# Short matrix products split in two within each period: adapters and weighted values first, output projection, then scores and mixing

## The chip, the cores and the metric

The kernel runs on one core of a Trainium2 chip. The metric is the device time in microseconds of one execution on that core, median of several runs. The core has five engines that work side by side and wait for each other by semaphores: TensorE (PE, matrix products into PSUM banks; PEld is its loading of weights), VectorE (DVE), ScalarE (ACT), GpSimd (POOL) and SyncE (SP), which here issues nearly all transfers.

## The reference

All data are 32-bit floats. `x` holds 128 sequences of 32 tokens with 512 channels. What is computed, cut to its steps:

```python
h = einsum('bct,bcd->bdt', x, cond_weights[cond])      # mixes the 32 tokens of a sequence
q, k, v = split(clip(h @ w_qkv.T, -8, 8))              # 512 channels each
q, k = layernorm(q) * qw + qb, layernorm(k) * kw + kb
s = q @ k.T / 4 + alibi_bias, causal                   # 32 heads of 16 channels, within a sequence
x = x + (softmax(s) @ v) @ w_out.T
h = x @ adapt_w[adapter].T                             # one 512x512 matrix for each sequence
gs = sum(top2(h @ gate_w))
y = relu(h @ up_w)**2 @ down_w + gs * (h @ fc1_w @ expert_w @ fc2_w)
out = x + layernorm(y) * gamma + beta
```

## The kernel before

The 4096 tokens are cut into 32 tiles of 128 tokens (`NTILE`), four sequences each; two neighbouring tiles make a pair (`GRP` = 2) for the feed-forward part. The loop at line 815 is software-pipelined by hand: one pass over its body is a period, and period t works on tile t + 2 (projections to q, k, v), tile t + 1 (scores, softmax), tile t (weighted values, output projection), tile t - 1 (adapter product), tile t - 2 (routing) and the pair before (up products in even t, down products in odd t). Tiles 0 to 3 are led in by the code from line 702 on.

In a period of the kernel before, TensorE's steps come in this order. The short ones use part of the array or few columns:

- `scores(t + 1)` (L439): 32 products on 64 rows x 32 columns of the array into the two banks `psc`; VectorE then adds the bias into `s`.
- `mix(t + 2)` (L301): from tile 5 on, 32 products on 64 x 32 into two banks `pxc` (the "parts"); ScalarE copies them to `xcT`. For the first tiles, `t <= 2 * GRP`, it is four 128 x 128 products into one bank instead.
- `adapt(t - 1)` (L559): 64 products on 128 x 32 into `pad`; VectorE transposes them to `hT`. The weights `adw` come by eight transfers of 512 KB (`load_adapters`, L255), which wait for `last_head`, the last such transpose.
- `weigh(t)` (L514): 32 products on 128 x 32 into `po`; VectorE transposes them to `aT`.

The rest is on the whole array, 128 x 128:

- `route(t - 2, 0)` (L585), four products into `pr`, from which `gs` and a part of `y` come;
- `fill(0)`, then `project(t + 2, 0)` and `project(t + 2, 1)` (q and k, L328) with `normalise` (L355) and `turn` (L402) behind them: `turn` transposes in blocks on VectorE, sends the blocks to memory and fetches them back turned, by one transfer `away_qk` and four `T_qk`;
- `attend(t)` (L536), the output projection `pw` from `aT`, which VectorE adds to `x`, and `turn_x(t)` (L549), which turns the new `x` the same way (`away_x`, four `T_x`) for the next period's `adapt` and lets GpSimd add beta to `x`;
- `fill(1)` to `fill(3)`, `project(t + 1, 2)` (v), `spread` (L499, GpSimd), `scale(t + 2)` (L413, ScalarE and VectorE, makes `kx` for the next period's scores), `route(t - 2, 1)`, `fill(4)` to `fill(7)`. One `fill` is four up products (`up`, L612, into `pu`) or two down products (`down`, L630, into `pd`). ScalarE applies relu to each `pu` and GpSimd squares it; VectorE adds `pd` to `y` (`total`, L641) and `finish` (L651) normalises.

The softmax is in `exponent` (L464: maximum on VectorE, subtraction on GpSimd, exp on ScalarE), `share` (L475: sum on VectorE, division on GpSimd) and `flip` (L487: transpose to `pT`, which `weigh` of the next period reads).

A 32-bit product of this kernel is two weight loads and two matmuls, four instructions, in TensorE's queue. The framework puts instructions in order for every engine by a schedule of its own; `after` (L77) fixes an order between two instructions of one engine without a wait. `short` chains all short products in the order of the code, and `queue` ties a long product behind the last instruction put there. `idle_instructions(n)` puts n instructions that do nothing behind the last product. `fill_up` calls it at seven places of a period, behind fill(0), the two projections, `attend` and fill(1) to fill(3); the seven share `FIRST` = 117 in period 2, and `SHORT` = 95 in even and 13 in odd periods:

```python
lack = FIRST if t == GRP else SHORT[t % GRP]
idle_instructions(lack // 7 + (i < lack % 7))
```

`last_scale` (L371, L434, L624) fixes one order on ScalarE: the relu of `fill(4)` comes behind the last scaling of q in `scale`.

Of the kernel before, what the change touches and what calls it, by code (L numbers as in the profile page):

```python
# [13 lines left out]
AF = mybir.ActivationFunctionType  # L14
# [3 lines left out]
P = 128  # L18
# [3 lines left out]
NTILE = NT // P  # L22
# [5 lines left out]
FC = INT // P  # L28
# [5 lines left out]
GRP = 2  # L34
ROUT = (0, NE + D // 2, NE + D)


SHORT = (95, 13)
FIRST = 117
CLIP = 8.0  # L40
EPS = 1e-5
NEG = -1.0e30
# [3 lines left out]
def adaln_attn_ffn(  # L46
# [22 lines left out]
    nc = tc.nc  # L69
# [4 lines left out]
    def bank(name):  # L74
        return ps.tile([P, 512], F32, tag="ps", name=name)

    def after(ins, first):  # L77

        tc.add_manual_dep(
            ins.ins, first.ins.name,  # L80
            mybir.DependencyInfo(mybir.DependencyClass.NoSync, mybir.DependencyReason.DATA),
            reason="order",
        )
# [10 lines left out]
    queue = []  # L94
    shorts = []

    def idle_instructions(n):

        for _ in range(n):
            nop = nc.tensor.nop("fill")  # L100
            after(nop, queue[-1])
            queue[:] = [nop]

    def product(*args, **kwargs):
        ins = nc.tensor.matmul(*args, **kwargs)  # L105
        if queue:
            after(ins, queue.pop())
        return ins

    def short(*args, **kwargs):  # L110

        ins = product(*args, **kwargs)
        if shorts:
            after(ins, shorts[-1])
        shorts[:] = [ins]
        return ins
# [184 lines left out]
    def mix(t):  # L301

        s = tiles[t]
        s["xcT"] = w2.tile([P, DC, P], F32, tag="xcT", name=f"xcT_{t}")
        blk = s["blk"].rearrange("p a b -> p (a b)")
        if t <= 2 * GRP:
            pxc = bank(f"pxc_{t}")
            for c in range(DC):
                nc.tensor.matmul(  # L309
                    pxc[:, ts(c, P)], lhsT=s["x"][:, ts(c, P)], rhs=blk, start=True, stop=True  # L310
                )
            nc.scalar.copy(s["xcT"].rearrange("p c n -> p (c n)"), pxc)
            return

        n = P // 2
        banks = [bank(f"pxc_{t}_{r}").rearrange("p (c n) -> p c n", c=DC) for r in range(2)]
        for c in range(DC):
            for g in range(DC):
                for r in range(2):
                    short(  # L320
                        banks[r][ts(g, S), c, :n],
                        lhsT=s["x"][ts(r, n), c * P + g * S : c * P + (g + 1) * S],
                        rhs=blk[ts(r, n), ts(r, n)], start=True, stop=True,
                    )
        for r in range(2):
            nc.scalar.copy(s["xcT"][:, :, ts(r, n)], banks[r][:, :, :n])
# [41 lines left out]

    last_flip = []
    last_head = []  # L370
    last_scale = []  # L371

    def swap(srcs, name):

# [38 lines left out]
    def scale(t):  # L413

        s = tiles[t]
        q, k = s["T"][:, :, 0], s["T"][:, :, 1]

        s["kx"] = w1.tile([P, DC, SEQ, HQ, S], F32, tag="kx", name=f"kx_{t}")
        for c in range(DC):
            nc.scalar.activation(  # L420
                k[:, :, c], s["raw"][1][:, :, c], AF.Identity,
                bias=lnc[:, 3, c : c + 1], scale=lnc[:, 2, c : c + 1],
            )
            kx = nc.vector.tensor_tensor(  # L424
                out=s["kx"][:, c],
                in0=k[:, :, c].unsqueeze(2).broadcast_to([P, SEQ, HQ, S]),
                in1=m_half.unsqueeze(1).unsqueeze(3).broadcast_to([P, SEQ, HQ, S]),
                op=ALU.mult,
            )

            if c == 0 and last_flip:
                after(kx, last_flip[-1])
        for c in range(DC):
            last_scale[:] = [nc.scalar.activation(  # L434
                q[:, :, c], s["raw"][0][:, :, c], AF.Identity,
                bias=qaff[:, 1, c : c + 1], scale=qaff[:, 0, c : c + 1],
            )]

    def scores(t):  # L439

# [171 lines left out]
    def up(g, f):  # L612

        pair = pairs[g]
        pu = bank(f"pu_{g}_{f}")
        for c in range(DC):
            last = product(
                pu[:, : GRP * P], lhsT=up_sb[:, c, ts(f, P)], rhs=pair["hT"][:, c, :],
                start=(c == 0), stop=(c == DC - 1),
            )  # L620
        a = hp.tile([P, GRP * P], F32, tag="act", name=f"act_{g}_{f}")
        relu = nc.scalar.activation(a, pu[:, : GRP * P], AF.Relu)  # L622

        if f == FC // 2 and last_scale:  # L624
            after(relu, last_scale.pop())
        nc.gpsimd.tensor_tensor(out=a, in0=a, in1=a, op=ALU.mult)  # L626
        pair["acts"].append(a)
        return last

    def down(t, quarter):  # L630
        s = tiles[t]
        if quarter == 0:
            s["pd"] = bank(f"pd_{t}")
        for f in range(2 * quarter, 2 * quarter + 2):
            last = product(
                s["pd"], lhsT=pairs[t // GRP]["acts"][f][:, ts(t % GRP, P)],
                rhs=down_sb[:, f, :], start=(f == 0), stop=(f == FC - 1),
            )
        return last
# [74 lines left out]
    routed_outer(0)  # L714
    routed_outer(1)
    mix(0)
    routed_outer(2)
    for c in range(DC):
        for i in range(2):
            project(0, i, (c,))  # L720
    normalise(0)
    mix(1)
    project(0, 2)
    wqkv_dma = dma
# [29 lines left out]
    project(1, 0)  # L754
    turn(0)
    scale(0)
    spread(0)
    project(1, 1)
# [3 lines left out]
    routed_outer(3)  # L762
    blend(2)
    mix(2)
    turn(1)
    project(1, 2)
    share(0)
    project(2, 0)
    scale(1)
    flip(0)  # L770
    blend(3)
# [14 lines left out]
    project(3, 0)  # L786
    share(1)
    scale(2)
    adapt(0)
    flip(1)  # L790
# [18 lines left out]
    def when(ok, step, *args):  # L809
        if ok:  # L810
            step(*args)
# [3 lines left out]
    for t in range(GRP, NTILE + GRP):  # L815
        here, ahead, two = t < NTILE, t + 1 < NTILE, t + 2 < NTILE
        g = t // GRP - 1

        def fill(i):
            last = up(g, i) if t % GRP == 0 else down(g * GRP + i // 4, i % 4)  # L820
            queue[:] = [last]
            if i < 4:
                fill_up(i)

        def fill_up(i):

            if here:
                lack = FIRST if t == GRP else SHORT[t % GRP]
                idle_instructions(lack // 7 + (i < lack % 7))

        when(t == GRP, adapt, t - 1)
        when(ahead, scores, t + 1)
        when(two and t > GRP, mix, t + 2)
        when(GRP < t <= NTILE, adapt, t - 1)
        when(here and t > GRP, weigh, t)
        when(ahead, exponent, t + 1)
        if here:


            load_adapters(t, last_head[-1])  # L840
        if t == GRP:
            after(
                nc.sync.dma_start(out=gam_sb, in_=gamma.broadcast_to([P, D])),
                last_adapter_dma[-1],
            )
        when(t + 3 < NTILE, load, t + 3)
        when(t > GRP and t % GRP == 0, finish, t - GRP - 1)
        when(t > GRP, route, t - GRP, 0)
        when(t == GRP, mix, t + 2)
        fill(0)  # L850
        when(two, project, t + 2, 0)
        fill_up(4)
        when(ahead, share, t + 1)
        when(t + 3 < NTILE, gather, t + 3)
        when(two, project, t + 2, 1)
        fill_up(5)
        when(ahead, flip, t + 1)
        when(two, normalise, t + 2)
        when(two, turn, t + 2)
        when(here, attend, t)  # L860
        fill_up(6)
        when(here, turn_x, t)
        fill(1)
        fill(2)
        fill(3)
        when(t % GRP, total, g * GRP)
        when(ahead, project, t + 1, 2)
        when(ahead, spread, t + 1)
        when(t + 3 < NTILE, blend, t + 3)
        when(t % GRP, finish, g * GRP)  # L870
        when(two, scale, t + 2)
        when(t > GRP, route, t - GRP, 1)
        if t == NTILE + GRP - 1:
            close(NTILE - 1)
            break
        for i in range(4, 8):
            fill(i)
        when(t % GRP, total, g * GRP + 1)
# [77 lines left out]
```

## Time and profile before

| what | us |
|---|---|
| median of 3 runs | 1236.95 (1235.41 to 1237.29) |
| the profiled execution | 1238.49 |
| its span, first to last instruction | 1236.7 |
| TensorE matmuls busy | 1226.7 (99%) |
| weight loads, which lie beside matmuls | 792.1 (64%) |
| VectorE busy | 685.1 (55%) |
| GpSimd busy | 456.9 (37%) |
| ScalarE busy | 330.4 (27%) |
| granted TensorE clock, mean | 0.999 of full |

The profile gives for each group of instructions its engine, the line of the code, output and inputs by name, the shape, how many, the busy time and the idle time before it with what ended that. Matmuls overlap by their run-in and run-out, so the distance from one start to the next tells more than a duration. "issue" as the end of an idle time means that no semaphore and no transfer of the profile ended it.

The largest groups on TensorE are the projections `pqkv` (340.3 us in 768 matmuls), `pu` (228.7), `pd` (220.4), `pr` (125.8), `pad` (121.3 in 4096), `pw` (115.3), `po` (38.3 in 2048), `psc` (37.3 in 2048) and `pxc` in parts (24.5 in 1728). A period takes a little over 37 us.

### The profile page before, as it was taken

What the parts mean: (1) busy time and instruction counts of PE and PEld (TensorE: products, weight loads), DVE (VectorE), ACT (ScalarE), POOL (GpSimd) and SP (SyncE); (2) the same over time, 40 slices, a digit from 0 to 9 for tenths busy, and PEclk for the clock granted to TensorE, in tenths of its full rate; (3) what the DMA queues carried; (4) which work ended last, traced back from release to release, by engine and by line L of the source; (5) the groups of instructions that cost most, each with busy time, mean ns of one, the idle gap of its engine ahead of it and who ended that gap; (6) DMA issues with size and microseconds to landing.
All of it is one profiled execution on the core that took longest, in us unless ns stands there. A gap on an engine that the chain in (4) does not pass through costs nothing.

```text
span 1236.7 us, 32576 instructions
## 1 busy us (share of the span) xinstructions
PE 1226.7 (99%) x13126; PEld 792.1 (64%) x13126; DVE 685.1 (55%) x1090; ACT 330.4 (27%) x675; POOL 456.9 (37%) x393
## 2 busy tenths in 40 slices
PE   9999999999999999999999999999999999999998
PEld 5576566674666756567665666746667566675765
DVE  2975555655556565564645646455565655656222
ACT  2433223231222322133222232222323222231111
POOL 3435334443333524234343343433344243342410
PEclk9999999999999999999999999999999999999999
DMA  9754544335544345544355443455443554533440
GB/s 281 222 196 169 205 189 164 133 135 205 206 165 171 119 165 206 192 169 146 116 202 206 180 167 119 152 206 204 149 159 123 190 205 177 180 114 141 176 157 18
DMA packets 93430, 209.53 MB, mean 169 GB/s; under 512 B 11749, under 2 KB 42470, under 8 KB 93286
## 3 DMA queue, kind: packets, MB, share of 16 engines
q1 hardware_dynamic: 89142, 198.39, 45.3%
q0 software_dynamic: 3424, 8.39, 1.8%
q8 instruction: 110, 1.80, 0.6%
q10 hardware_dynamic: 720, 0.66, 0.2%
q14 instruction: 34, 0.28, 0.1%
HBM read 176.47 MB, written 30.93 MB: 168 GB/s over the span
## 4 chain that ended last, share of the span: by engine, by line
PE 99%; DMA 0%; issue 0%; DVE 0%; ACTq 0%; DVEq 0%
PE pqkv L105 27%; PE pu L105 18%; PE pd L105 17%; PE pad L105 10%; PE pr L592 10%; PE pw L105 9%; PE psc L105 3%; PE po L105 3%; PE pxc L105 2%; PE pro L216 1%; PE pd L676 1%; DMA fc_t<-in_fc_w 0%; PE pxc L309 0%; PE pt L399 0%; PE pe L206 0%
## 5 line engine op out<-in xcount | busy, mean ns | idle before, releaser
L105 PE MATMUL pqkv<-wqkv_sb,xcT 128*128 128x512 f32 x768 | 340.3, 592 | 0.0
L105 PEld LDWEIGHTS pqkv<-wqkv_sb,xcT 128*128 128x128 f32 x768 | 145.5, 190 | 168.6 <-issue 159.0
L105 PE MATMUL pu<-hT,up_sb 128*128 128x256 f32 x1024 | 228.7, 379 | 0.0
L105 PE MATMUL pd<-down_sb,act 128*128 128x512 f32 x496 | 220.4, 592 | 0.0
L105 PEld LDWEIGHTS pu<-hT,up_sb 128*128 128x128 f32 x1024 | 194.5, 190 | 33.4 <-issue 7.7
L424 DVE TENSOR_TENSOR kx<-T_qk,m_half 128x512 f32<-128x512 f32 x128 | 138.0, 1137 | 55.8 <-ACT T_qk L420 55.8
L105 PEld LDWEIGHTS pd<-down_sb,act 128*128 128x128 f32 x496 | 94.2, 190 | 105.6 <-issue 103.6
L505 POOL TENSOR_TENSOR vx<-v,msk 128x1024 f32<-128x1024 f32 x64 | 134.3, 2123 | 59.9 <-DVE v L346 51.2
L468 POOL TENSOR_TENSOR s<-s,mx 128x1024 f32<-128x1024 f32 x32 | 67.1, 2097 | 169.6 <-DVE mx L467 169.6
L592 PE MATMUL pr<-rout_sb,hT 128*128 128x256 f32 (+1 forms) x512 | 125.8, 389 | 0.0
L105 PE MATMUL pad<-adw,T_x 128*32 128x128 f32 x4096 | 121.3, 273 | 2.4 <-issue 1.8
L626 POOL TENSOR_TENSOR act<-act 128x256 f32<-128x256 f32 x128 | 89.8, 710 | 88.7 <-ACT act L622 88.5
L105 PEld LDWEIGHTS pad<-adw,T_x 128*32 128x32 f32 x4096 | 111.3, 110 | 9.2 <-issue 6.0
L105 PE MATMUL pw<-wout_sb,aT 128*128 128x512 f32 x256 | 115.3, 593 | 0.0
L592 PEld LDWEIGHTS pr<-rout_sb,hT 128*128 128x128 f32 x512 | 94.7, 190 | 29.0 <-issue 15.0
L483 POOL TENSOR_TENSOR s<-s,rden 128x1024 f32<-128x1024 f32 x32 | 61.3, 1916 | 89.5 <-DVE gs L601 80.5
L346 DVE TENSOR_SCALAR qk<-pqkv 128x512 f32<-128x512 f32 x64 | 44.1, 689 | 78.6 <-PE pqkv L105 78.2
L105 PEld LDWEIGHTS pw<-wout_sb,aT 128*128 128x128 f32 x256 | 48.5, 190 | 60.9 <-issue 60.4
L557 POOL TENSOR_TENSOR x<-x,bet_sb 128x512 f32<-128x512 f32 x32 | 40.7, 1273 | 119.0 <-DVE blocks_x L380 116.7
L622 ACT ACTIVATE act<-pu 128x256 f32<-128x256 f32 x128 | 47.0, 379 | 136.3 <-PE pu L105 136.3
L491 DVE STREAM_TRANSPOSE pT<-s 128x1024 f32<-128x1024 f32 x32 | 39.8, 1245 | 61.1 <-POOL s L483 61.1
L294 POOL TENSOR_TENSOR blk<-cw,msk 128x128 f32<-128x128 f32 x32 | 12.8, 401 | 150.6 <-DMA cw<-in_cond_w,rows 135.6
(79 smaller groups left out, 1074.5 us busy)
## 6 DMA issues: line engine op xcount, KB each, us to landing
adw<-in_adapt_w SPq DMA_DIRECT2D x256, 512.0 KB, 7.8
away_qk<-blocks_qk SPq DMA_DIRECT2D x28, 512.0 KB, 2.6
T_qk<-away_qk SPq DMA_DIRECT2D x112, 128.0 KB, 2.9
x<-in_x SPq DMA_DIRECT2D x32, 256.0 KB, 10.4
away_x<-blocks_x SPq DMA_DIRECT2D x30, 256.0 KB, 2.7
T_x<-away_x SPq DMA_DIRECT2D x120, 64.0 KB, 2.5
out<-y POOLq DMA_DIRECT2D x30, 256.0 KB, 2.8
wqkv_sb<-in_w_qkvT SPq DMA_DIRECT2D x12, 256.0 KB, 5.6
```

Source lines behind the costliest of these rows:

```text
L105: ins = nc.tensor.matmul(*args, **kwargs)
L294: nc.gpsimd.tensor_tensor(out=s["blk"], in0=s["cw"].unsqueeze(1).broadcast_to([P, SEQ, S]), in1=m_seq.unsqueeze(2).broadcast_to([P, SEQ, S ...
L346: nc.vector.tensor_scalar(out=s["qk"][:, i, :] if i < 2 else s["v"], in0=s["pp", i], scalar1=-CLIP, scalar2=CLIP, op0=ALU.max, op1=ALU.min,)
L424: kx = nc.vector.tensor_tensor(out=s["kx"][:, c], in0=k[:, :, c].unsqueeze(2).broadcast_to([P, SEQ, HQ, S]), in1=m_half.unsqueeze(1).unsqu ...
L468: nc.gpsimd.tensor_tensor(out=s["s"], in0=s["s"], in1=mx.unsqueeze(2).broadcast_to([P, H, S]), op=ALU.subtract,)
L483: s["shared"] = nc.gpsimd.tensor_tensor(out=s["s"], in0=s["s"], in1=rden.unsqueeze(2).broadcast_to([P, H, S]), op=ALU.mult)
L491: pT = nc.vector.transpose(out=s["pT"].rearrange("p h q -> p (h q)"), in_=s["s"].rearrange("p h k -> p (h k)"),)
L505: nc.gpsimd.tensor_tensor(out=vx, in0=s["v"][:, ts(half, D // 2)].rearrange("p (h d) -> p h d", d=HD).unsqueeze(2) .broadcast_to([P, H // ...
L557: nc.gpsimd.tensor_tensor(out=s["x"], in0=s["x"], in1=bet_sb, op=ALU.add)
L592: nc.tensor.matmul(pr[:, :n], lhsT=hT[:, c, ts(t % GRP, P)], rhs=rout_sb[:, c, ROUT[half] : ROUT[half + 1]], start=(c == 0), stop=(c == DC ...
L622: relu = nc.scalar.activation(a, pu[:, : GRP * P], AF.Relu)
L626: nc.gpsimd.tensor_tensor(out=a, in0=a, in1=a, op=ALU.mult)
```

## The change

Period t now begins with `adapt(t - 1)` and `weigh(t)`; `route(t - 2, 0)` follows, then `attend(t)` and `turn_x(t)`, which move up from behind the projections; then `scores(t + 1)`, `mix(t + 2)` and `exponent(t + 1)`, and behind these fill(0) and the rest in the old order. The special order of period 2 goes, but for one tie: there `attend` is placed behind the last short product. `mix` works in parts from tile 4 on, not from tile 5. The idle instructions are shared among six places (the one behind `attend` is gone): none in period 2, 57 in even and 58 in odd periods. `last_scale` goes.

```diff
-SHORT = (95, 13)
-FIRST = 117
+SHORT = (57, 58)
+FIRST = 0
...
-        if t <= 2 * GRP:
+        if t < 2 * GRP:
...
-    last_scale = []
...
-            last_scale[:] = [nc.scalar.activation(
+            nc.scalar.activation(
                 q[:, :, c], s["raw"][0][:, :, c], AF.Identity,
                 bias=qaff[:, 1, c : c + 1], scale=qaff[:, 0, c : c + 1],
-            )]
+            )
...
-        relu = nc.scalar.activation(a, pu[:, : GRP * P], AF.Relu)
-
-        if f == FC // 2 and last_scale:
-            after(relu, last_scale.pop())
+        nc.scalar.activation(a, pu[:, : GRP * P], AF.Relu)
...
-                idle_instructions(lack // 7 + (i < lack % 7))
-
-        when(t == GRP, adapt, t - 1)
-        when(ahead, scores, t + 1)
-        when(two and t > GRP, mix, t + 2)
-        when(GRP < t <= NTILE, adapt, t - 1)
+                idle_instructions(lack // 6 + (i < lack % 6))
+
+        when(t <= NTILE, adapt, t - 1)
         when(here and t > GRP, weigh, t)
-        when(ahead, exponent, t + 1)
         if here:
...
             load_adapters(t, last_head[-1])
...
         when(t > GRP and t % GRP == 0, finish, t - GRP - 1)
         when(t > GRP, route, t - GRP, 0)
-        when(t == GRP, mix, t + 2)
+        if t == GRP:
+            queue[:] = [shorts[-1]]
+        when(here, attend, t)
+        when(here, turn_x, t)
+        when(ahead, scores, t + 1)
+        when(two, mix, t + 2)
+        when(ahead, exponent, t + 1)
         fill(0)
         when(two, project, t + 2, 0)
         fill_up(4)
...
         when(two, turn, t + 2)
-        when(here, attend, t)
-        fill_up(6)
-        when(here, turn_x, t)
         fill(1)
```

## The prediction

> **What bounds the kernel now.** I read the page's busy times and chain first, then the periods of the loop one by one, then TensorE's order of time inside a period.
>
> ```profile
> PE 1226.7 (99%) x13126; PEld 792.1 (64%) x13126; DVE 685.1 (55%) x1090; ACT 330.4 (27%) x675; POOL 456.9 (37%) x393
> ...
> q8 instruction: 110, 1.80, 0.6%
> ...
> PE 99%; DMA 0%; issue 0%; DVE 0%; ACTq 0%; DVEq 0%
> ```
>
> TensorE is the chain, almost without a break; no other engine passes 55%. So only two things can move the time: spaces between TensorE's own instructions, and a wait that does not exist today. The second row returns below. Next the periods, cut at each first `psc` (scores), which in this kernel opens a period:
>
> ```profile
> 571.13:608.56 37.43, 37.43 (x402) 21.19 (x401) 21.46 (x34) 9.27 (x18) 12.01 (x9) 1.00 0.48 170
> 533.43:571.13 37.70, 37.70 (x434) 27.40 (x433) 21.75 (x34) 11.11 (x24) 16.82 (x15) 1.00 0.48 170
> 117.08:156.88 39.80, 38.02 (x401) 21.26 (x401) 21.96 (x35) 9.27 (x18) 13.49 (x11) 1.00 0.45 160
> ```
>
> The second column is the length. 37.43 us is the shortest, met again and again for odd and even t: I call it clean. The 27 periods from t = 3 (117.08) to t = 29 (ending 1136.74) take 1019.66 us, 27 x 37.43 = 1010.61, so 9.05 us are lost: 2.37 in t = 3, 0.70 in t = 4, 5.98 in the other 25. That is all the change can win in the loop.
>
> ```profile
> 117.08 1.16 PE L105 MATMUL psc<-kx,T_qk 64*32 64x128 f32 x64
> 117.98 0.91 PE L105 MATMUL pxc<-blk,x 64*32 64x64 f32 x64
> 118.82 0.42 PE L105 MATMUL pad<-adw,T_x 128*32 128x128 f32 x6
> 120.99 3.57 PE L105 MATMUL pad<-adw,T_x 128*32 128x128 f32 x121 [1.75 <-issue]
> ```
>
> **Where the 9.05 us go.** In t = 3 the adapter products stop after six, released by "issue": no engine, no DMA. I numbered the records of TensorE's queue in order of start. This stop is at record 2498; others, of 0.1 to 0.4 us, are at 3522, 4545, 10690, 14274, 17858. All leave 193 or 194 when divided by 256. The instruction queue's 110 packets of 1.80 MB are 16.4 KB each, one for 256 of the queue's 28,213 records. The packet before the big stop starts at 118.76 and work resumes 2.23 us later; at 463.07 and 613.58 it is 2.38 and 2.46. The adapter weights had landed by 103.2 and `T_x` by 112.8, so once the block is in time nothing is late behind it. So a stop is an instruction block that comes late: 256 records that run through in under some 3.4 to 3.9 us (117.1 to 120.99; 274 to 530 records after the first `psc` in the usual odd period) outrun the next. Today one period begins with 640 dense records (scores 128, mix 128, adapters 256, weigh 128) in 6.3 us, so two block borders always lie close.
>
> Beside the Trainium skill's page "Runtime: NRT & Kernel Launch", section "Instruction fetch mechanics", this row disagrees: the page says blocks of 256 instructions stream in and crossing a border is mostly hidden. By the page the stops would be nothing, the change would win nothing and the estimate would be some 7 us higher.
>
> **The idle instructions.** Odd t has 400 loads, 400 matmuls, 13 idle, 11 waits = 824 records; even t 432 + 432 + 95 + 9 = 968; together 1792 = 7 x 256, so borders stay put. Afterwards 1664 + 115 = 1779; with 13 waits that is 1792 again, and I assume it. The first `pad` of t = 2 starts at record 1510. The changed t = 2 holds adapters 256, output projection 16, scores 128, mix 128, products 176, no idle ones, some 8 waits: 712. So t = 3 begins at 2222 and its borders are 20, 276 and 532 records in; even periods, about 865 later, have them at 180, 436, 692. 20 to 276 looks close, but in the usual odd period today a border 18 records into `psc` starts its packet 2.3 us ahead of the first `psc` (493.66 against 496.00), since the queue is read ahead during long matmuls. 276 to 532 and 180 to 436 now hold routing and output projection (1.88 + 3.43 us). I expect no full stop. Borders inside dense work still cost 0.10 to 0.15 (`pxc` to `pad` 0.25 instead of 0.145 in several even periods); two such in 14 odd periods, at 0.06 on average, 1.7 us. Bounds: 0 to 6.0, today's loss kept. An idle instruction takes 0.071 us of the queue; ten behind fill(0) are 0.7 us under 1.72 us of matmuls, hence nothing. At t = 30, where no projection separates the places, today's 40 take 2.9 us, and `pu` and `pw` run 0.23 long (1.88 for 1.73, 3.51 for 3.43); 29 take 2.0, so 0.23 is won.
>
> **The extra split.** Removing nothing from TensorE, the change cuts the dense run in two, and small array shapes are entered and left twice.
>
> ```profile
> 526.47 7.03 PE L105 MATMUL pd<-down_sb,act 128*128 128x512 f32 x16
> 533.43 1.16 PE L105 MATMUL psc<-kx,T_qk 64*32 64x128 f32 x64
> 534.32 0.91 PE L105 MATMUL pxc<-blk,x 64*32 64x64 f32 x64
> 535.16 3.78 PE L105 MATMUL pad<-adw,T_x 128*32 128x128 f32 x125
> ...
> 539.88 2.05 PE L592 MATMUL pr<-rout_sb,hT 128*128 128x264 f32 x8
> 541.76 1.89 PE L105 MATMUL pu<-hT,up_sb 128*128 128x256 f32 x8
> 543.49 7.03 PE L105 MATMUL pqkv<-wqkv_sb,xcT 128*128 128x512 f32 x16
> 550.35 3.60 PE L105 MATMUL pw<-wout_sb,aT 128*128 128x512 f32 x8
> ```
>
> Read differences of starts. Entering: `pd` x16 takes 6.96 where 16 long ones take 6.86, so 0.09 (0.522 instead of 0.429 at the last). 64x32 to 128x32: the last `pxc` to `pad` takes 0.145 instead of about 0.01: 0.14. Leaving: the last `po` to `pr` takes 0.15, and `pr` needs 1.88 where 1.73 x 264/256 = 1.78 would do: 0.10 more. Afterwards, entering at `pad` costs the 0.09 that `psc` costs today; `pad`, `po`, `pr` are as now; new are entering at `psc` (0.09) and leaving after `pxc` (0.25, taken from `po`, which is also 64 wide; gone is its 0.14). Sum +0.20 us a period, 29 periods (t = 2 to 30): +5.8. No row shows `pxc` to fill(0): leaving the wider `psc` for the big `pxc` at 88.4 cost 0.30, so the upper end is 0.25 a period, 7.3; at the lower the leaving is free, 0.09 - 0.14 = -0.05, -1.5. I take 0.20, by the row of equal width.
>
> The Trainium skill, "TensorEngine Tiling (Array Packing)", section "Key Properties", states that changing the tiling mode drains the engine. It speaks against this change; it gives no figure, so the rows above price it. By rule and by row one more leaving and entering is paid.
>
> **The moved steps, queue by queue.** Zero below counts from the first `pad`.
>
> ```profile
> 576.63 0.72 DVE L578 STREAM_TRANSPOSE hT<-pad 128x512 f32<-128x512 f32 x1 [1.76 <-PE pad L105]
> 577.52 0.72 DVE L529 STREAM_TRANSPOSE aT<-po 128x512 f32<-128x512 f32 x1 [0.17 <-PE po L105]
> ```
>
> *Output projection* (8 matmuls, 3.43) needs `aT`, 0.72 us of VectorE after the last `po`; today project covers it for 10 us, afterwards only `pr`, 2.03 from the last `po`. It is ready about 1.0 after that, so it costs 0 with 0.6 to spare for the weight load. *turn_x*: VectorE add 0.69 and transpose 0.67 run at about 10.1, before the scores come; SP's `away_x` queues behind the eight adapter loads (the last of them lands 13.7 us after the first issue) and holds SP until about 20; SP's next client, `away_qk`, comes at about 26, and `T_x` is needed at 37.6. GpSimd's add, 1.27, ends before the maximum. All hidden. *Scores and exponent*: adds 1.28, maximum 1.22, GpSimd 1.91, exp 1.06, sum 1.22, GpSimd 1.91, transpose 1.25 end near 22; weigh needs them at 41. They delay normalise by some 3 us against today, so `T_qk` lands near 33.5 and `kx` ends near 37 to 39; scores wait until 47.8. *Mix*: two ScalarE copies, 0.65, against fill(0), 1.82: 0. The `last_scale` order goes; whichever of relu and scale comes first, scores have 9 us. Bounds of all this: 0, and what the second rival prices.
>
> **Sum.** The profiled execution took 1238.49, span 1236.7. Lost blocks -9.05, border costs +1.7, switching +5.8, idle at t = 30 -0.23: -1.8. I add 0.3 for waits too small to name: -1.5. That is 1237.0 for a like execution; the median stands 1.54 below the profiled one, so 1236.95 - 1.5 = **1235.4 us**. Its own range, from switching at 4.4 to 7.3 and borders at 0 to 3: 1232.3 to 1238.2.
>
> **Rivals.** *Borders free, leaving cheaper*: fill(0) pays only the 0.15 gap, not the slow second load, so 0.10 a period, 2.9; borders cost 0. For it speaks the read-ahead; against it, that every row leaving 32-wide shapes shows the 0.10 as well. -9.05 - 0.23 + 2.9 = -6.4: 1230.6. *`aT` comes late* (slower): `kx` of the next tile, at the end of a period, ends past the start of the next; in even periods VectorE then adds the last down product (y, statistics, two row steps: 3.0 us) before `hT` and `aT`. If `kx` ends more than 1.3 us after the first `pad`, `aT` passes 6.2 and `pw` waits. For it: `kx` has taken 4.2 us beside GpSimd work (2.38 for one of four at 528.16). Against: scores leave little GpSimd work there. At 0.5 us in 14 even periods and 0.1 in odd ones 8.4: 1243.8. *Borders elsewhere*: if the waits are not 13, the borders drift through the dense part and the stops stay at 6.0: 1235.4 - 1.7 + 6.0 = 1239.7 (1241 with a big one as in t = 3).
>
> **Chances.** Forecast 0.48, cheaper leaving 0.14, late `aT` 0.20, borders elsewhere 0.18. About 0.2% (2.5 us) is what a measurement of this kernel tells from no change: below 1234.5 is faster, above 1239.4 slower. The forecast's case puts 0.17 below, 0.27 between and 0.04 above; cheaper leaving 0.14 below; late `aT` 0.02 between, 0.18 above; borders 0.05 between, 0.13 above. Faster 0.31, same 0.34, slower 0.35. The range runs from 1231.0, just above cheaper leaving, to 1244, late `aT`: about 0.1 lies outside on each side.
>
> **What would show it.** Right: a clean period near 37.63; no `pad` stop at t = 3; `pw` starting 1.88 after `pr`; 0.25 after `pxc`; `aT` at most 0.1 after `po` ends. Wrong: gaps at `pw` released by VectorE's `aT`, gaps at `pqkv` released by ScalarE's `xcT`, or "issue" stops of 0.3 and more in `po` or `psc`.

## The result and the profile after

The changed kernel takes 1245.48 us (median of 4 runs, 1245.01 to 1247.08), the kernel before 1236.94 beside it: a ratio of 1.0071, 95% interval 1.0059 to 1.0084. It is slower by 0.7%, 10.1 us above the forecast and 1.5 above the upper end of the range. The profiled execution took 1247.08, span 1245.3.

The page of the kernel after, first busy times, then the instruction queue (packets, MB, share), then who holds the chain that ended last:

```profile
PE 1231.7 (99%) x13182; PEld 785.4 (63%) x13182; DVE 629.1 (51%) x1090; ACT 333.6 (27%) x676; POOL 431.8 (35%) x393
...
q8 instruction: 110, 1.80, 0.6%
...
PE 62%; DVE 18%; DMA 7%; ACT 5%; POOL 4%; issue 3%; SPq 1%; ACTq 0%; DVEq 0%; POOLq 0%
```

VectorE is less busy than before (55% then) and yet holds 18% of the chain, where it held none. Something on TensorE now waits for it. Two neighbouring periods in the view by windows of the kernel after, an odd one and an even one, cut at the first `pad` (columns: length, then busy time and count of PE, PEld, DVE, ACT, POOL, granted clock, DMA share, GB/s):

```profile
497.78:535.41 37.63, 37.63 (x401) 21.11 (x401) 18.90 (x34) 11.11 (x23) 11.50 (x9) 1.00 0.46 169
535.41:573.68 38.27, 37.98 (x433) 27.11 (x433) 20.29 (x36) 9.51 (x20) 15.48 (x15) 1.00 0.45 167
```

Every odd period takes the forecast's clean 37.63. The even ones take 38.27 to 38.54. In the even one the timeline of TensorE shows where (start, length, instruction, count, idle before):

```profile
539.93 2.05 PE L591 MATMUL pr<-rout_sb,hT 128*128 128x264 f32 x8
542.28 3.70 PE L105 MATMUL pw<-wout_sb,aT 128*128 128x512 f32 x8 [0.29 <-DVE top L598]
545.91 1.16 PE L105 MATMUL psc<-kx,T_qk 64*32 64x128 f32 x64
```

From the first `pr` to the first `pw` it is 2.35 us instead of 1.88, from there to `psc` 3.63 instead of 3.53: 0.57 lost. `top` is only the last thing VectorE had finished; what `pw` needs is `aT`. VectorE's timeline of the same stretch, in which the odd period ends at 535.41:

```profile
527.66 0.69 DVE L346 TENSOR_SCALAR v<-pqkv 128x512 f32<-128x512 f32 x1
535.57 0.69 DVE L641 TENSOR_TENSOR y<-y,pd 128x512 f32<-128x512 f32 x1 [7.23 <-ACT T_qk L433]
536.18 2.49 DVE L423 TENSOR_TENSOR kx<-T_qk,m_half 128x512 f32<-128x512 f32 x4
538.59 0.69 DVE L643 BATCH_NORM_STATS2 stf<-y 128x6 f32<-128x512 f32 x1
...
539.52 0.75 DVE L652 SCALAR_TENSOR_TENSOR y<-y,mvf,gam_sb 128x512 f32<-128x512 f32 x1
540.19 0.16 DVE L227 RECIPROCAL rstd_f<-std_f 128x1 f32<-128x1 f32 x1
540.27 0.70 DVE L577 STREAM_TRANSPOSE hT<-pad 128x512 f32<-128x512 f32 x1
540.89 0.71 DVE L655 SCALAR_TENSOR_TENSOR y<-y,rstd_f,x 128x512 f32<-128x512 f32 x1
541.51 0.71 DVE L528 STREAM_TRANSPOSE aT<-po 128x512 f32<-128x512 f32 x1
```

`y`, the total of the odd tile, needs the last down product, that is the end of the period, and VectorE stands idle for it. (The 7.23 us are put down to the last scaling of q, which ended at about the same time.) `T_qk` had landed at 532.10 and ScalarE scaled k from 532.21, but the four `kx` stand *behind* `y`. So they, the statistics and the two row steps fall into the first 6 us of the even period, and `aT` ends at 542.22, where `pr` would have let `pw` start at 541.81. In the kernel before, `kx` stood ahead of `y` and ended at 531.76, before that period's end at 533.43:

```profile
527.56 4.20 DVE L424 TENSOR_TENSOR kx<-T_qk,m_half 128x512 f32<-128x512 f32 x4 [1.92 <-ACT T_qk L420]
533.53 0.69 DVE L645 TENSOR_TENSOR y<-y,pd 128x512 f32<-128x512 f32 x1 [1.78 <-PE pd L105]
```

No stop released by "issue" is left in the loop. Over the 27 periods from t = 3 the kernel after takes 1025.83 us (before: 1019.66).

### The profile page after: what moved, and what is told of

Read it like the earlier page. It is cut to its first block, busy times and chain, and to the rows that moved or that the text cites. A ratio compares the mean times of both kernels' runs of the same rounds, so it can differ in the third digit from the quotient of the medians.

```text
span 1245.3 us, 32639 instructions
## 1 busy us (share of the span) xinstructions
PE 1231.7 (99%) x13182; PEld 785.4 (63%) x13182; DVE 629.1 (51%) x1090; ACT 333.6 (27%) x676; POOL 431.8 (35%) x393
## 4 chain that ended last, share of the span: by engine, by line
PE 62%; DVE 18%; DMA 7%; ACT 5%; POOL 4%; issue 3%; SPq 1%; ACTq 0%; DVEq 0%; POOLq 0%
PE pu L105 18%; PE pqkv L105 16%; PE pw L105 9%; PE pr L591 5%; PE pad L105 5%; DMA T_qk<-away_qk 4%; DVE kx L423 3%; PE pd L105 3%; DMA away_qk<-blocks_qk 3%; POOL s L467 2%; POOL s L482 2%; ACT T_qk L419 2%; PE psc L105 2%; ACT T_qk L433 2%; PE po L105 1%
## 5 line engine op out<-in xcount | busy, mean ns | idle before, releaser
L504 POOL TENSOR_TENSOR vx<-v,msk 128x1024 f32<-128x1024 f32 x64 | 120.0, 1901 | 58.0 <-DVE v L346 49.4
L423 DVE TENSOR_TENSOR kx<-T_qk,m_half 128x512 f32<-128x512 f32 x128 | 86.4, 734 | 100.1 <-ACT T_qk L419 100.1
L105 PE MATMUL pad<-adw,T_x 128*32 128x128 f32 x4096 | 118.8, 273 | 0.1
L622 POOL TENSOR_TENSOR act<-act 128x256 f32<-128x256 f32 x128 | 84.1, 664 | 81.8 <-ACT act L621 81.3
L659 POOL DMA_DIRECT2D out<-y x30 | 18.2, 605 | 235.7 <-DVE y L655 119.1
L477 DVE TENSOR_REDUCE den<-s 128x32 f32<-128x1024 f32 x32 | 39.0, 1220 | 94.2 <-ACT s L472 94.2
L641 DVE TENSOR_TENSOR y<-y,pd 128x512 f32<-128x512 f32 x31 | 20.8, 670 | 118.5 <-ACT T_qk L433 93.9
L467 POOL TENSOR_TENSOR s<-s,mx 128x1024 f32<-128x1024 f32 x32 | 61.8, 1932 | 37.2 <-DVE mx L466 37.2
```

The source lines that it names most:

```text
L423: kx = nc.vector.tensor_tensor(out=s["kx"][:, c], in0=k[:, :, c].unsqueeze(2).broadcast_to([P, SEQ, HQ, S]), in1=m_half.unsqueeze(1).unsqu ...
L467: nc.gpsimd.tensor_tensor(out=s["s"], in0=s["s"], in1=mx.unsqueeze(2).broadcast_to([P, H, S]), op=ALU.subtract,)
L477: total = nc.vector.tensor_reduce(out=den, in_=s["s"], axis=AX.X, op=ALU.add)
L504: nc.gpsimd.tensor_tensor(out=vx, in0=s["v"][:, ts(half, D // 2)].rearrange("p (h d) -> p h d", d=HD).unsqueeze(2) .broadcast_to([P, H // ...
```

## The experiments

Each was run beside the kernel before on the same chip; the ratios are to that. "..." marks lines left out of an edit.

**VectorE's order.** First: the total behind the last `kx` (odd tiles).

```diff
+    last_kx = []
...
+        last_kx[:] = [kx]
...
-        nc.vector.tensor_tensor(out=y, in0=y, in1=s["pd"], op=ALU.add)
+        add = nc.vector.tensor_tensor(out=y, in0=y, in1=s["pd"], op=ALU.add)
+        if t % GRP and t + 3 < NTILE:
+            after(add, last_kx[-1])
```

> Theory 1 (VectorE's order): in odd periods after the change VectorE waits 8.5 us for the last down product with the total y, and the four kx multiplications (0.685 each, 2.74 in all) stand behind it, so hT and aT of the next, even period come late: pr takes 2.35 instead of 1.88 and pw 3.63 instead of 3.53. With y behind the last kx, kx runs in the odd period's own last 4 us and y starts at its end: even periods fall from 38.27 to about 37.7 and the time by 8 to 9 us, to about 1236.8. Theory 2 (blocks): the excess of the even periods is a block border behind fill(0); then they stay above 38.1 and the time at 1244 to 1246. Theory 3 (aT is simply too late, whatever the order: kx itself ends late because the scaled keys come late): kx would end no earlier than 1.3 us after the first pad, even periods 38.2 and the time 1244 to 1246.

Measured: 1235.7 us (1235.43 to 1236.28), ratio 0.9967 (0.9955 to 0.9979): 9.8 us below the changed kernel and 0.3% faster than the kernel before, which took 1239.88 beside it. Its windows and VectorE's timeline, same tiles:

```profile
493.94:531.56 37.62, 37.62 (x401) 21.11 (x400) 21.33 (x37) 10.88 (x23) 11.49 (x9) 1.00 0.47 169
531.56:569.27 37.71, 37.71 (x433) 27.19 (x433) 18.33 (x33) 9.72 (x21) 15.47 (x15) 1.00 0.48 169
```

```profile
529.11 2.50 DVE L424 TENSOR_TENSOR kx<-T_qk,m_half 128x512 f32<-128x512 f32 x4 [4.61 <-ACT T_qk L420]
531.67 0.69 DVE L643 TENSOR_TENSOR y<-y,pd 128x512 f32<-128x512 f32 x1
...
535.33 0.72 DVE L579 STREAM_TRANSPOSE hT<-pad 128x512 f32<-128x512 f32 x1 [1.24 <-PE pad L105]
...
536.80 0.71 DVE L530 STREAM_TRANSPOSE aT<-po 128x512 f32<-128x512 f32 x1
```

`kx` runs inside the 7.2 us that VectorE had stood idle, ends 0.05 us after the odd period, and `hT` waits for TensorE, not the other way round. All 13 even periods from t = 4 to 28 take 37.71, the 27 periods 1016.96.

Second: `y` stays ahead of `kx`, but its row steps are tied behind `hT` (`last_head`); in the trace they came behind `aT` too.

```diff
-        nc.vector.scalar_tensor_tensor(
+        row = nc.vector.scalar_tensor_tensor(
             out=y, in0=y, scalar=mv[:, 0, 0:1], in1=gam_sb, op0=ALU.subtract, op1=ALU.mult
         )
+        if t % GRP:
+            after(row, last_head[-1])
```

> The total y stays ahead of kx, but its two row steps (0.62 and 0.68, 1.3 us together) go behind aT in the odd tiles. Theory 1 (what VectorE has in front of aT is too long): aT comes some 1.3 us sooner than 542.2, pw waits no more, even periods 37.65 to 37.8, time 1236.5 to 1238. Theory 2 (blocks) and a theory that the wait for the product itself is what hurts: no change, 1244 to 1246.

Measured: 1236.03 us, ratio 0.9971 (0.9959 to 0.9983). VectorE's timeline:

```profile
530.54 0.69 DVE L641 TENSOR_TENSOR y<-y,pd 128x512 f32<-128x512 f32 x1 [7.22 <-ACT T_qk L433]
531.14 2.49 DVE L423 TENSOR_TENSOR kx<-T_qk,m_half 128x512 f32<-128x512 f32 x4
...
535.52 0.68 DVE L528 STREAM_TRANSPOSE aT<-po 128x512 f32<-128x512 f32 x1
536.12 0.71 DVE L652 SCALAR_TENSOR_TENSOR y<-y,mvf,gam_sb 128x512 f32<-128x512 f32 x1
```

The same wait for the period's end, the same late `kx`, and still every period is 37.63 or 37.71: `aT` starts 5.15 us into the period instead of 6.10. So the wait for `y` by itself costs nothing; what costs is all that VectorE then has ahead of `aT`.

Third, a rival: ScalarE's dropped order is brought back.

```diff
+            last_scale[:] = [nc.scalar.activation(
...
+        relu = nc.scalar.activation(a, pu[:, : GRP * P], AF.Relu)
+        if f == FC // 2 and last_scale:
+            after(relu, last_scale.pop())
```

> The relu of fill 4 is ordered behind the last scaling again, as in the kernel before; nothing else. Rival theory (the order that the change dropped is the cause: relu now runs ahead of the scaling of k, so kx is late): kx moves ahead of y and the time falls by 6 to 9 us, to 1236 to 1239. Theory 1: in the trace ScalarE scales k at 532.2, 0.1 us after T_qk lands at 532.1, and VectorE is already waiting for the last down product from 527.0, so nothing changes: 1244.5 to 1246.5, even periods 38.2 to 38.3.

Measured: 1245.45 us, ratio 1.0046 (1.003 to 1.0061), the changed kernel's own time. The group of `pw` still waits (busy, mean ns, then idle before and its end):

```profile
L105 PE MATMUL pw<-wout_sb,aT 128*128 128x512 f32 x256 | 116.7, 599 | 4.2 <-DVE top L599 4.2
```

Dropping `last_scale` was free, as forecast.

**Where the order came from.** `attend` and `turn_x` go back behind the projections; the rest of the change stays.

```diff
-        when(here, attend, t)
-        when(here, turn_x, t)
         when(ahead, scores, t + 1)
...
         when(two, turn, t + 2)
+        when(here, attend, t)
+        when(here, turn_x, t)
```

> Attend and the turn of x go back to their old place behind both parts of project; everything else of the change stays, and nothing is said of VectorE's order. Theory 1, with its origin: the 3.43 of the output projection ahead of project is what made qk, T_qk and so kx late enough for VectorE's order to put y first; with attend back, T_qk lands some 3.4 us sooner, kx stands ahead of y again by itself, ends about 1.5 us before the period does, and no matmul waits for VectorE. Rival (the later scores and exponent, not the output projection, put kx behind): y stays ahead of kx. Time: without the output projection, routing, scores, mix and fill(0) follow one another closely, 256 records from record 437 to 693 of an even period in about 2.3 us, so block stops of 0 to 2 us are possible in 14 even periods: 1236 to 1264, all of the excess released by issue and none by VectorE.

Measured: 1312.6 us, ratio 1.0589 (1.0555 to 1.0622). VectorE's timeline around the end of an odd period (312.74), the table of waits of TensorE (total, times, longest), and the granted clock in tenths, in 40 slices of the execution:

```profile
306.86 4.20 DVE L423 TENSOR_TENSOR kx<-T_qk,m_half 128x512 f32<-128x512 f32 x4 [1.92 <-ACT T_qk L419]
312.84 0.69 DVE L641 TENSOR_TENSOR y<-y,pd 128x512 f32<-128x512 f32 x1 [1.79 <-PE pd L105]
...
317.40 0.72 DVE L528 STREAM_TRANSPOSE aT<-po 128x512 f32<-128x512 f32 x1 [0.18 <-PE po L105]
```

```profile
PE pxc L105 <- issue: 29.2, 8, 5.0
PE pu L105 <- issue: 11.1, 3, 5.0
PE pqkv L105 <- issue: 4.7, 3, 2.6
...
PEclk9999999999999989989899898998989999999999
```

On VectorE the theory holds: nothing was said of the order, and `kx` is ahead of `y` again. `T_qk` lands 30.9 us into the odd period instead of 34.3; the 3.4 us are the output projection (8 matmuls, 3.43). Scores and exponent stand where the change put them, so they are not the cause. What the framework's schedule goes by isn't shown, only that the order turns with the place of `attend`. The time fell far outside the expectation: without the output projection in between, an even period loses 2 to 7 us, not 0 to 2. The stops at instruction blocks are 1.9 to 5.0 us of that. At ten of the thirteen the granted clock then stands at 0.5 for 3.41 or 6.83 us (`pqkv` x16 behind one of them takes 8.08 instead of 6.87). In the 27 periods TensorE stands idle for 48.3 of the 73.3 us that they take more than in the first experiment; most of the rest is this slower clock (44.0 us of matmuls ran at 0.5, some 22 lost by this estimate).

**More cover for `aT` in another way:** scores and mix between routing and the output projection.

```diff
-        when(here, attend, t)
-        when(here, turn_x, t)
         when(ahead, scores, t + 1)
         when(two, mix, t + 2)
         when(ahead, exponent, t + 1)
+        queue[:] = [shorts[-1]]
+        when(here, attend, t)
+        when(here, turn_x, t)
```

> Attend (the output projection) and the turn of x go behind scores and mix, ahead of fill(0); VectorE's order of y and kx is untouched. The number of changes of array shape stays the same. Theory 1: scores and mix (0.9 and 0.84 us) now lie between routing and the output projection, more than the 0.57 to 0.64 by which aT is late, so pw no longer waits; but the VectorE adds of the scores may slip in ahead of aT, 1.28 us. Even and odd periods about 37.6 to 37.8, time 1236.5 to 1238.5. Theory 2 (the even periods lose their time to a block border or to routing's own reads): no change, or worse, 1244 to 1248, since adapters, routing, scores and mix stand closer together again.

Measured: 1267.48 us, ratio 1.0231 (1.019 to 1.0272): a miss. Up to t = 9 all periods take 37.63 or 37.72, so `aT` is covered, as theory 1 had it. Then even periods grow to as much as 44.5, all but t = 22 and 26; at four of the stops the granted clock falls to 0.5 for 3.41 us. One of them, on TensorE:

```profile
542.86 0.87 PE L105 MATMUL pxc<-blk,x 64*32 64x64 f32 x60
546.17 0.30 PE L105 MATMUL pxc<-blk,x 64*32 64x64 f32 x4 [2.44 <-issue]
```

Two periods are 1799 records here, so the block borders move 7 records ahead in each pair of periods, and the stop moves along: behind product 60, 57, 53, 50, 43 and 36 of `pxc`, always at a record that leaves 193 or 194 when divided by 256.

**The split and the borders.** On the first experiment's kernel, scores, mix and exponent go up to directly behind the weighted values.

```diff
         when(here and t > GRP, weigh, t)
+        when(ahead, scores, t + 1)
+        when(two, mix, t + 2)
+        when(ahead, exponent, t + 1)
```

(Their three calls behind `turn_x` go.)

> The first experiment's kernel (1235.7) with scores, mix and the exponent moved up to directly behind the weighted values, ahead of routing: adapters, values, scores and mix are one run of 640 dense records, and array shapes are entered and left once. Prediction's term: the second entering and leaving costs 0.20 a period, 29 periods, so without blocks 1229.9. Theory of the blocks: the borders stay at 22, 278, 534 and 181, 437, 693, and 278 to 534 (1.9 us) and 181 to 437 (2.4 us) outrun the next block: stops of 0.7 to 1.6 us in each period, 1248 to 1275. Rival (a border costs next to nothing): 1229 to 1232.

Measured: 1267.77 us, ratio 1.023 (1.0212 to 1.0248). A stop in nearly every period, here in t = 3:

```profile
123.77 0.29 PE L105 MATMUL pxc<-blk,x 64*32 64x64 f32 x7
125.09 0.79 PE L105 MATMUL pxc<-blk,x 64*32 64x64 f32 x57 [1.03 <-issue]
```

The 27 periods take 1044.90. Both terms can be read: `pw` x8 takes 3.43 instead of 3.53 and fill(0) 1.72 or 1.73 instead of 1.82 or 1.83, which is the 0.20 of the second change of shapes; 1016.96 - 27 x 0.20 = 1011.6, so stops cost 33.3 us, 1.2 a period, within the 0.7 to 1.6 expected. (The borders did not stay put as written there: two periods were 1799 records.)

Then the borders alone: `FIRST = 100` on the first experiment's kernel.

> The first experiment's kernel (1235.7) with 100 idle instructions in period t = 2 instead of none, which moves every later block border 100 records ahead: from 22, 278, 534 of odd and 181, 437, 693 of even periods to 178, 434, 690 and 81, 337, 593. Theory of the blocks: 81 to 337 of an even period are adapters and half the weighted values, 3.05 us, so a stop of 0.3 to 0.8 in each of 14 even periods, plus up to 7 us at t = 2 for the idle instructions themselves where they are not hidden: 1240 to 1248. Rival (borders are hidden wherever they lie, and the clean periods come from VectorE's order alone): no change in the periods, 1235 to 1237, or up to 7 more from t = 2 alone.

Measured: 1236.4 us, ratio 0.9974 (0.9964 to 0.9984). The borders moved as computed; the 27 periods take 1017.75. In the 13 even periods, where the stretch lies, they cost nothing in nine, 0.02 to 0.07 in three and 0.62 in one. The expectation of 0.3 to 0.8 each fell: 256 records in 3.05 us are nearly always free here, where only one such stretch comes at a time.

No idle instructions at all: `SHORT = (0, 0)`, so that the borders wander.

> The first experiment's kernel (1235.7) without any idle instruction in the loop: two periods are 1677 records instead of 1792, no multiple of 256, so the block borders stand 115 records earlier in each pair of periods and come to lie everywhere once. Theory A (what frees the periods of stops is that two runs of 384 and 256 dense records are 5.4 us of long matmuls apart, wherever borders lie, as the 100 records of the last experiment moved them at no cost): a stop under 0.5 us in a few periods at most, 1234.5 to 1238; the packet starts at the border and the block is usable 2.3 to 3 us later, and the fastest 256 records take 2.7 us. Theory B (the idle instructions keep the borders at places that happen to be good): stops of 0.5 to 2 us in about a third of the periods, 1240 to 1252.

Measured: 1238.77 us, ratio 0.9987 (0.9977 to 0.9996), between the two theories, nearer A: stops of 0.1 to 0.9 us in 8 of 27 periods, 4.1 us together by the trace. The pinned borders of the change are thus worth some 3 us (2.5 by the two ratios, as the runs are from different chips).

**Why some borders stop.** On that kernel the adapter loads go behind the exponent and wait for its maximum; the loads of gamma and of the next `x`, which stand behind them, move along.

```diff
-            load_adapters(t, last_head[-1])
...
         when(ahead, exponent, t + 1)
+        if here:
+            load_adapters(t, tiles[t + 1]["mx"] if ahead else last_head[-1])
...
```

> The last experiment's kernel (no idle instructions, 1238.8, stops in 8 of 27 periods) with the eight adapter loads and the load of x behind the exponent, waiting for the maximum of the scores, some 6 us later. There the block packet that had not started by 5.3 us into a period started only at 8.3 to 9.7, and the adapters' first packets start at 7.0. Theory C (the block packet is held up by the adapter loads): it now starts when the border is passed, the stops in mix go, 1235 to 1236.5. Rival (its start is set by something else, such as how far TensorE's queue is read ahead): packets at 8.3 to 9.7 and stops remain, 1238 to 1240. Should the loads come too late for the next adapters (they took to 21.8 us of 37.6, so would end near 29), a wait before pad would show it.

Measured: 1237.78 us, ratio 0.9998 (0.9988 to 1.0007). The same period with the same borders, without and with the later loads:

```profile
240.83 0.62 PE L105 MATMUL pxc<-blk,x 64*32 64x64 f32 x32
241.63 0.46 PE L105 MATMUL pxc<-blk,x 64*32 64x64 f32 x32 [0.18 <-issue]
```

```profile
241.28 0.91 PE L105 MATMUL pxc<-blk,x 64*32 64x64 f32 x64
```

The loads are issued from 16.6 us into the period on, not from 6.0, and no other transfer of that queue starts before 12.3. All five stops in `pxc` are gone, and of six in `po` one of 0.3 us is left (these lie ahead of any load; why they went too isn't shown). Theory C holds for the packets of the `pxc` stops. That it shortens the run isn't shown: the medians differ by 1.0 us, but they are from different chips and the intervals of the ratios overlap; t = 3 also lost 1.24 us, with `kx` late there.

Last, the joined run with late loads and borders meant to be pinned (`SHORT = (54, 54)`, `FIRST = 52`):

> The joined run of 640 dense records (1267.8) with the adapter loads behind the exponent as in the other run of this pair, and idle instructions set (54 and 54, 52 at t = 2) so that two periods are 1792 records and borders stand at 128, 384, 640 of even and 225, 481, 737 of odd periods. Theory C, with a block usable 2.3 us after its packet starts: stops of 0 to 0.6 us a period and one change of shapes less, 1230 to 1245, at best under the first experiment's 1235.7. Rival (640 dense records in 6.3 us outrun the blocks whatever the loads do): stops of 1 to 2 us in most periods as before, 1255 to 1270.

Measured: 1262.17 us, ratio 1.0204 (1.0184 to 1.0223): the rival. Two periods were 1790 records, so the borders moved by two in each pair. The 27 periods take 1040.59, 29.0 over the 1011.6 without stops, 1.1 a period. The kernel before has 640 dense records in a row too, scores and mix first, and loses 8.0 in 27 periods, 0.3 each; whether their order or the places of its borders spares it was not run. Starts of instruction packets, in us from the first `pad`, from the traces of six even periods (borders in records from that `pad`):

```
kernel           borders        packets at     lost
borders moved    81 337 593     1.18  4.95     none
no idle          98 354 610     1.68  9.53     0.4 in po and pxc
late loads       98 354 610     1.67  5.15     none
joined, late    135 391 647     2.07  6.08     1.8 in pr
attend late     142 398 654     2.14  7.74     2.7 in pxc
attend back     158 414 670     2.31 12.14     5.9 in fill(0)
```

In ten traces (before, after and eight of the runs) no two packets start less than 3.19 us apart, whatever TensorE does. In the first and third row the second packet starts 0.9 and 1.0 us after its border is passed. In the second and the last it starts 5.3 and 5.6 us after; there the adapters' first packets start at 7.0 and 6.4, and in these six rows only there ahead of it. How the loads hold it up the traces don't show: in the second row the border is passed 2.7 us ahead of the loads' first packet. In the fourth and fifth row it starts 1.3 and 2.0 us after with no load under way (first packets at 9.7 and 7.9): why, isn't settled.

Paired in order with the borders of the 27 periods, 33 of 89 packets start over 2 us after their border in the run without idle instructions, and 4 of 89 with the loads late. But 27 of 95 do in the first experiment's kernel, which has no stop; and in the changed kernel the packet at 11.01, behind the loads' first packets at 7.8, starts 0.5 us after its border. So neither does the load alone make a packet late, nor a late packet alone a stop.

## Why the prediction was wrong

**The step that failed** is the one on the moved output projection: "It is ready about 1.0 after that, so it costs 0 with 0.6 to spare for the weight load." This took `aT` to follow `po` as it did in the kernel before, when VectorE had nothing else to do there. Measured: 0.56 a period in the 14 even periods from t = 4 to 30, 7.9 us; with VectorE's order mended, 0. The step before it had the cause in hand: it put `T_qk` at 33.5 and the end of `kx` near 37 to 39, the very end of a period of 37.63, and asked only whether the scores would wait. What a late `kx` does to VectorE's order at the start of the next period it left to the second rival, and put into the sum at nothing. It also gave the delay to scores and exponent. `T_qk` landed 34.3 us into the odd period, 30.3 in the kernel before; the run with `attend` back, 30.9, shows that the output projection, 3.43 us moved ahead of the projections to q and k, made 3.4 of these 4.0. It followed the moved steps through the queues of SP and GpSimd, and not through VectorE's own, behind the projections that they delay.

**The rival "`aT` comes late"** had the place (`pw` in even periods), the price (0.5 for 0.56 measured) and nearly the time (1243.8 for 1245.48), at a chance of 0.20. Its reason was off by one: it let `kx` run late and `y` follow; in fact `y` waits for the period's end and `kx` follows. Its "against", little GpSimd work beside `kx`, was true and beside the point: `kx` took 2.49, not 4.2, and was late all the same.

**Border costs** were put at 1.7 us inside dense work. In the changed kernel 1.5 us were lost, but behind fill(0) of eight even periods (up to 0.18 there and 0.07 in the next), where the second packet started 11.1 to 11.5 us in; once `aT` was in time it started at 10.0 to 10.5, and nothing was lost. A by-product of the wait, then.

**The places of the borders** were right: forecast 20, 276, 532 and 180, 436, 692; measured 22, 278, 534 and 181, 437, 693, and two periods of exactly 1792 records. "No full stop" was right from t = 3 on. "A stop is an instruction block that comes late" was right, and the runs with moving borders show it; but the limit, 256 records in under 3.4 to 3.9 us, is that of several blocks in a row, as the packets' spacing of 3.19 and more tells; a single block in 3.05 was free in nine of 13 periods.

**The extra split**, 0.20 a period, was right in odd and even periods, by taking it back too.

**The clean period** was wrong for even t: 37.43 was never met there; its 64 up matmuls take 0.08 more than the 32 down ones of an odd period (32 up take 6.91 and 24 take 5.18, where 16 down take 6.87 and 12 take 5.15), which makes it 37.51 (37.71 afterwards). Of the 9.05 us called lost, 13 x 0.08 = 1.0 could not be won.

**In sum** the loop was forecast at -1.95 against before and took +6.17, 8.1 apart: 7.3 for `aT` in 13 even periods, 1.0 for the even clean period, -0.2 for borders. The other 2.0 of the 10.1 between the profiled executions are t = 30 (0.6, `aT` again), the start (0.5) and the time behind the last matmul (1.1; the other three runs of the changed kernel lie 1.5 to 2.1 below the profiled one), less the 0.3 added for small waits. The kernel with `kx` first, 1235.7, has the order that the forecast of 1235.4 described, but the near match is luck in part. Its loop took 2.70 us less than before, not 1.95: no border costs instead of 1.7, against the 1.0 that could not be won. And the kernel before beside it took 1239.88, not 1236.95.

On the page "Runtime: NRT & Kernel Launch" of the Trainium skill, section "Instruction fetch mechanics", crossing a block is mostly hidden. The kernel with `kx` first agrees, no stop in 27 periods; the one with `attend` back doesn't, up to 5.0 us at one border. The measurement decides: it depends on what runs between two borders, and on the loads beside them.

## What to carry to other kernels

When a long step is moved ahead of another on the engine that bounds, everything behind the other moves back by its length: follow that to the end of the period on every engine, and look whether an instruction that waits for the period's end now comes ahead of work that the next period needs early. Where a framework makes the order, a small move can turn it over; one tie (`kx` before `y`) was worth 9.8 us here, more than the change could win. Spread dense short instructions so that long ones lie between them, before tuning where the blocks end.

## What was not expected of the hardware

- Instruction packets were never less than 3.19 us apart in ten traces. A run of 640 records in 6.3 us, two borders at least, lost 1.2 and 1.1 us a period in the two joined kernels, and 0.3 in the kernel before.
- In one kernel a packet started 5.3 us after its border, behind the first packets of eight 512 KB loads; with the loads issued from 16.6 instead of 6.0 us into the period on, it started 1.0 us after the same border, and the stops in `pxc` were gone.
- A single stretch of 256 records in 3.05 us cost nothing in nine of 13 periods, and more than 0.07 us in one.
- A long stop can cost more than itself. In the four runs with `attend` late, `attend` back and the joined steps, 26 stops lasted 1.86 us or more; at 16 of them the granted clock fell to 0.5 for 3.41 or 6.83 us, from within the stop or up to 1.4 us behind it, and at none of the shorter ones. Why ten were spared isn't shown.
